# A two-layer convolution and attention network on eight images: position terms of the first image's keys formed without the round trip through DRAM, and its pieces in another order

## The chip, the cores and the metric

The kernel runs on one core of one Trainium2 chip. A core has TensorE (PE, matrix products; its weight loads are shown as PEld), VectorE (DVE, elementwise), ScalarE (ACT, activations and copies), GpSimd (POOL, elementwise by a general processor), SyncE (SP, which here issues most DMAs), sixteen DMA engines, the on-chip memory SBUF and the matrix accumulator PSUM. The metric is the device time of one execution in microseconds (us), lower is better.

## The reference, cut to what matters

Input x is 8 images of 512 channels by 32 x 32, fp32. Layer 0 group-normalises the image, takes a 1x1 convolution to 512 channels (cv1), sends the second half of these through two blocks, each a 3x3 convolution and an attention over the 1024 pixels with four heads of 64 channels, joins everything in a 1x1 convolution (cv2) and adds the input. Layer 1 group-normalises again, takes a depthwise 3x3 and a 1x1 convolution and adds its input. The part that the change touches is the position term r in the attention's keys:

```python
q, k, v = (qkv[:, 0], qkv[:, 1], qkv[:, 2])
r = (rw + rh).reshape(1, HEADS, HD, hw)
logits = jnp.einsum('bhdi,bhdj->bhij', q, k + r) * HD ** (-0.5)
a = jax.nn.softmax(logits, axis=-1)
out = jnp.einsum('bhij,bhdj->bhdi', a, v)
```

rw has one value for each channel and column, rh one for each channel and line, so r is a 1024-element row for each of 256 channels, the same for all eight images. It exists once for each of the two blocks.

## The kernel before, in words

**Staging.** One image is worked on at a time, with all of its 512 channels as four tiles of 128 partitions by 1024 pixels. The pixels lie in "phases": four groups by column modulo 4. All arithmetic is fp32.

**The 3x3 convolutions** are done by a transform method. Weights are transformed once, in the first image: pieces `ta0`, `ta1`, `ta2` make "uplanes" from the raw weights (DVE for 0 and 1, ACT for 2), `ti0`..`ti2` combine them (DVE, tiles `ucomp`) and store them to DRAM (`u_dram`, by SP), `to0`..`to2` scale and store the outer ones (ACT, its own DMA queue). The raw weights of block 0 wait in the tiles `qy`, `kr` and `vt`, those of block 1 in `ht` and `xt`. Then, for every image and block: `d` transforms the input along and across rows (DVE, tiles `vtmp`, `v`, and then `kr`, `vt`, `qy` as the three groups of components), `P` multiplies (six pieces of 32 products, PSUM tiles `ps_c`), `Rc`, `R`, `B`, `E` transform back (ACT copies `c`, DVE tiles `mid`, `sd`, `y`) and `Ez` writes z. `P` takes its transformed weights from a ring of five 1 MB tiles (`wring`); a new ring load is issued on SP when a tile has been used (`ring_load`, `rl`).

**Query, key, value.** `k`, `v` and `q` are products of z with the ring's weights. `ka` (`add_positions`) adds the position rows to the keys while it takes them out of PSUM: DVE reads `ps_qk` and `kr` and writes `kr`. For this `kd` (`load_positions`) has loaded both position tiles from DRAM into `kr`. They come from `rk` (`positions`, line 880 on): four pieces, made in the first image by GpSimd (line 886) and stored by SP to `r_dram`.

**Attention.** 32 steps in a block. In each, `s` makes scores (PSUM `ps_s`, eight matmul instructions), `e` is ACT's exponential into a tile `e`, `p` adds it to `sum` on DVE, `w` multiplies it with the values (`ps_av`). `h` and `z` join halves, `n` and `nr` make the reciprocals of the sums, `ns` spreads them (a DMA, `rw<-r`), `sc` scales z. `m`, `ma`, `mr` close the block, `Q` is the cv2 product.

**Other first-image work.** In the first image's second attention the cv2 and layer-1 weights are combined for later images (`cw`: `combine_more` and `combine_weights`): a load into `ht`, sums on DVE (tiles `scomb`), stores by SP (`q<-ht`, `q<-scomb`, `s<-ht`, `s<-scomb`). `g`..`ga` are group norms, `fo` folds the batch norms.

**What sets the order.** The order is written out by hand. `FIRST` holds the first image's pieces, `HEAD` and `TAIL` those of images 2 to 7, `HEAD` and `LAST` those of image 8. `go` calls them in turn. PE, DVE, ACT and SP are wrapped in `InOrder` (line 94; its calls are recorded at line 104), so each of these four runs its instructions in exactly that order; GpSimd is free within its dependencies. An instruction that waits therefore holds everything behind it on its engine. Temporary tiles (`uplane`, `wtmp`, `ucomp`, `pos`, `scomb`, `e`, `sum`, `mid` and more) share one pool of 11 buffers of 512 KB; a new tile waits until the last reader of an old one is done, and for a stored tile that is its DMA.

Of the kernel before, what the change touches and what calls it, by code (L numbers as in the profile page):

```python
# [12 lines left out]
ALU = mybir.AluOpType  # L13
AX = mybir.AxisListType

P = 128
B, C, F = 8, 512, 32
# [25 lines left out]


FIRST = """
    g*5 gm gd g*2 gv g gp gm gd gb ga gv ga c gp fo gb ga ta0 ga ta0*2 ti0 ta2 fo ta2 c to0 ti0
    to0 c ti0 ta2 c rk*2 rl ca rk ta1*3 rk y ya ti1 ca ti2 to2 ti1*2 y to1 ya ti2 to1 d y*2 ti2
    d*2 ya d to2 rl P Rc d*2 R d*2 P d Rc d kd R d P Rc R ya B d P B P Rc R Rc R P E B Ez B Rc R
    E Ez X ta0 dw k*3 ka k ta0 ka ta0 ti0*2 v ta1 ti0 v*2 q va q qa v va q ta1*2 q qa s e s e p
    to0 s e w to0 s e w*2 p ti1*2 s e p ti1 p s e p w s*2 ta2 e p w e w to1*2 s e w s e p w h p  # L50
    z s ta2 e p ta2 s e ti2 w p w s w e p ti2 s e w p ti2 to2 s*2 e p w to2 e w s e p w s e p rh
    w h z s*2 w e*2 n nr p w s e p w nr s e p w s nr e nc s nr e ns w s p e w*2 p nc s e p w h z
    s p e p s w s*2 e w p e p w sc s e p w*2 e sc s e w*3 h p*2 n z nr*4 ns Q nc*2 K sc dp sc m
    ma mr m ma m*2 ma*2 mr*3 Q d*4 K P*2 kd Rc d*3 R d*3 Rc R d*2 P Rc R B P Rc P Rc R B*2 R E
    Ez B P Rc R E Ez k X k dx k*2 ka v ka v q v*2 va*2 q qa q*2 qa s*2 e s w e p s e p e w s p e
    cw*4 s e w s e p w p s e s p w s p e*2 w cw*2 w*2 p s w h e w z s p s e*2 p w s p g cw e s e
    w s w s p e g p g s w s p e w e g p w g e p h z s w e p s cw*2 w e p n nr*3 w s g e s p w nr
    e s e p s w e ns w g w s e w p h p s e p nc*2 s w e p w s e w s p sc e w s p e p s e p w sc
    w*3 h z*2 n nr Q*2 nr*2 g nr ns sc*2 nc m ma mr nc m ma m mr ma m ma mr gm gd mr Q*2 gv u A
    x u i A x gp i*3 Q gb ga*4 Q im id Q iv A x i ip Q i ib b bm t*2 Q t A x t i*2  # L60
"""

HEAD = """
# [20 lines left out]
"""  # L84

LAST = """
    Q sc*2 nc*2 m ma m*3 ma rg ma mr*2 ma mr*2 Q*2 A rg x i*2 Q im id iv ip ib b bm Q*3 t A x
    i*2 im id t*3 iv ip t ib Q t b Q bm t*3 A t l lr t Q x i*2 Q im lp id t iv ip t A ib t b bm
    Q t*2 A x t l lr x i*2 o lp o*3 im id t*2 o*3 iv ip t o*2 t ib b bm o*5 t o t*2 o t l t*2 lr
    lp t*3 o t*2 o*4 l o lr lp o*6 oa*2 fr f oa*2 fr f o*2 oa*2 o*2 fr oa f oa fr f  # L90
"""


# [31 lines left out]
def fast_kernel(  # L125
# [16 lines left out]
    nc = Engines(tc)  # L142
# [12 lines left out]
    def const_tile(shape, name):  # L155
        return const.tile(shape, F32, tag=name, name=name)

    def work_tile(name):
        return workp.tile([P, HW], F32, tag="work", name=name)

    def big_tile(name):
        return ps_big.tile([P, 2, 512], F32, tag="big", name=name)
# [33 lines left out]
    z = const_tile([P, 2, HW], "z")  # L196

    qy = const_tile([P, 2, HW], "qy")
    kr = const_tile([P, 2, HW], "kr")
# [54 lines left out]
    sc = const_tile([P, NBN], "sc")  # L254
# [19 lines left out]
    dw = v_sb[:, V_DW : V_DW + 9 * KC].rearrange("p (c t) -> p c t", t=9)  # L274
    rw = v_sb[:, V_RW : V_RW + 4 * F].rearrange("p (l m w) -> p l m w", l=2, w=F)
    rh = v_sb[:, V_RH : V_RH + 4 * F].rearrange("p (l m h) -> p l m h", l=2, h=F)
# [7 lines left out]
    def flat(ps):  # L284
        return ps.rearrange("p n f -> p (n f)")
# [5 lines left out]
    def phases(ap):  # L291

        return ap.rearrange("p (r h t) -> p r h t", h=F, t=F // 4)
# [12 lines left out]
    def add(name, *pieces):  # L306
        todo.setdefault(name, []).extend(pieces)
# [104 lines left out]
    def ring_load(n=1):  # L412
        for _ in range(n):
            if not sources:
                continue
            if holds and len(sources) <= holds[0]:
                waiting[0] += 1
                continue
            src = sources.pop(0)
            t = ringp.tile([P, 2048], F32, tag="ring", name="wring")  # L420
            o = t[:, : src[1]]
            if src[1] == 1024:
                o = o.rearrange("p (k o) -> p k o", o=P)
            nc.sync.dma_start(o, src[0])
            ring.append(t)
# [454 lines left out]
    def positions(l, m):  # L880

        t = work_tile("pos")
        full = [P, 4, F, F // 4]
        col = rw[:, l, m, :].rearrange("p (t r) -> p r t", r=4).unsqueeze(2)
        row = rh[:, l, m, :].unsqueeze(1).unsqueeze(3)
        nc.gpsimd.tensor_tensor(phases(t), col.to_broadcast(full), row.to_broadcast(full), ALU.add)
        nc.sync.dma_start(r_dram[l][:, m], t)

    def qkv(l, by_input):


        wt, tiles, values = [], {}, {}

        def weights():
            if not wt:
                wt.append(ring.pop(0)[:, : 6 * C2].rearrange("p (k o) -> p k o", k=2))
            return wt[0]

        def products(m, k):
            w = weights()  # L900
            if m not in tiles:
                tiles[m] = big_tile("ps_qk")
            for n in range(2):
                nc.tensor.matmul(
                    tiles[m][:, n, :],
                    w[:, k, m * P : (m + 1) * P],
                    z[:, k, n * 512 : (n + 1) * 512],
                    start=(k == 0),
                    stop=(k == 1),
                )  # L910

        def load_positions():
            nc.sync.dma_start(kr, r_dram[l])

        def add_positions(m):
            nc.vector.tensor_tensor(kr[:, m, :], flat(tiles.pop(m + 2)), kr[:, m, :], ALU.add)

        def value_products(g, js):
            w = weights()
            if g not in values:  # L920
                values[g] = ps_big.tile([P, 4, C2], F32, tag="big", name="ps_v")
            for j in js:
                jt = 4 * g + j
                for k in range(2):
                    nc.tensor.matmul(
                        values[g][:, j, :],
                        z[:, k, jt * P : (jt + 1) * P],
                        w[:, k, 2 * C2 : 3 * C2],
                        start=(k == 0),
                        stop=(k == 1),  # L930
                    )

        def value_end(g):
            nc.scalar.copy(vt[:, 4 * g : 4 * g + 4, :], values.pop(g))

        def query_end(m):
            nc.scalar.copy(qy[:, m, :], flat(tiles.pop(m)))

        order = [(k, m) for m in (2, 3) for k in range(2)]
        add("k", *[lambda m=m, k=k: products(m, k) for k, m in (sorted(order) if by_input else order)])  # L940
        add("kd", load_positions)
        add("ka", *[lambda m=m: add_positions(m) for m in range(2)])
        add("v", *[lambda g=g, j=j: value_products(g, (j, j + 1)) for g in range(2) for j in (0, 2)])
        add("va", *[lambda g=g: value_end(g) for g in range(2)])
        add("q", *[lambda m=m, k=k: products(m, k) for m in range(2) for k in range(2)])
        todo["q"].append(lambda last=todo["q"].pop(): (last(), ring_load()))
        add("qa", *[lambda m=m: query_end(m) for m in range(2)])
# [402 lines left out]
    for b in range(B):  # L1350
# [26 lines left out]
        for l in range(2):  # L1377
            conv3(l)
            qkv(l, first)
            attention()  # L1380
            cv2m(l)
# [471 lines left out]
```

## Time and profile before

| | us |
|---|---|
| median of 3 runs | 2611.19 |
| lowest, highest | 2610.63, 2613.28 |
| span of the profiled execution | 2610.8 |
| PE busy in it | 2561.2 (98%) |
| DVE busy | 2081.7 (80%) |
| ACT busy | 1185.3 (45%) |
| POOL busy | 101.7 (4%) |

PE is busy in nearly all of the span. An image in the middle takes PE without a break, and the time in which PE stands idle lies in the first image (its start, and its second attention) and at the end of the last one. So the stretches of the first image have to be read one by one: in each, which engine had work, what the idle one waited for, and what was queued ahead of that. The page's totals, and the group means over all images, hide this.

### The profile page before, as it was taken

What the parts mean: (1) busy time and instruction counts of PE and PEld (TensorE: products, weight loads), DVE (VectorE), ACT (ScalarE), POOL (GpSimd) and SP (SyncE); (2) the same over time, 40 slices, a digit from 0 to 9 for tenths busy, and PEclk for the clock granted to TensorE, in tenths of its full rate; (3) what the DMA queues carried; (4) which work ended last, traced back from release to release, by engine and by line L of the source; (5) the groups of instructions that cost most, each with busy time, mean ns of one, the idle gap of its engine ahead of it and who ended that gap; (6) DMA issues with size and microseconds to landing.
All of it is one profiled execution on the core that took longest, in us unless ns stands there. A gap on an engine that the chain in (4) does not pass through costs nothing.

```text
span 2610.8 us, 36350 instructions
## 1 busy us (share of the span) xinstructions
PE 2561.2 (98%) x14806; PEld 1292.4 (50%) x14806; DVE 2081.7 (80%) x2978; ACT 1185.3 (45%) x1523; POOL 101.7 (4%) x71
## 2 busy tenths in 40 slices
PE   6999999999999999999999999999999999999997
PEld 4554464544636346363464634646355453645443
DVE  8875678876898768987788877887788877888657
ACT  3544436353363533635446354453445444453534
POOL 3000001000000000000000000000000000000000
PEclk9999999999999999999999999999999999999999
DMA  8455230332304222151130601306122161312300
GB/s 329 154 200 188 66 136 25 112 143 65 121 25 165 99 73 105 33 209 54 65 122 17 246 17 65 122 17 246 33 77 93 38 225 33 129 42 93 113 17 33
DMA packets 82061, 270.59 MB, mean 104 GB/s; under 512 B 6880, under 2 KB 37344, under 8 KB 65632
## 3 DMA queue, kind: packets, MB, share of 16 engines
q1 hardware_dynamic: 78336, 264.79, 28.4%
q10 hardware_dynamic: 3552, 3.41, 0.4%
q8 instruction: 118, 1.93, 0.3%
q14 instruction: 55, 0.45, 0.0%
HBM read 214.44 MB, written 36.96 MB: 96 GB/s over the span
## 4 chain that ended last, share of the span: by engine, by line
PE 91%; DVE 6%; ACT 1%; DMA 1%; issue 0%; SPq 0%; POOL 0%; ACTq 0%; DVEq 0%
PE ps_av L104 17%; PE ps_s L104 16%; PE ps_c L104 12%; PE ps_cv L104 10%; PE ps_qk L104 8%; PE ps_cv2q L104 8%; PE ps_q L104 6%; PE ps_v L104 4%; PE ps_m L104 4%; PE ps_y L104 4%; PE ps_dn L104 1%; DVE ht L104 1%; ACT qy L104 1%; DVE vtmp L104 1%; DVE mid L104 1%; DVE uplane L104 0%
## 5 line engine op out<-in xcount | busy, mean ns | idle before, releaser
L104 ACT ACTIVATE e<-ps_s 128x1024 f32<-128x1024 f32 x512 | 509.5, 1023 | 291.5 <-PE ps_s L104 264.4
L104 PE MATMUL ps_s<-qy,kr 64*64 64x512 f32 x4096 | 514.9, 593 | 5.8 <-ACT e L104 4.4
L104 DVE TENSOR_TENSOR sum<-sum,e 128x1024 f32<-128x1024 f32 x384 | 475.6, 1239 | 41.5 <-ACT e L104 22.1
L104 PE MATMUL ps_av<-e,vt 64*64 64x512 f32 x4096 | 507.2, 591 | 0.0
L104 DVE SCALAR_TENSOR_TENSOR ht<-xn,v_sb,ht 128x961 f32<-128x961 f32 (+1 forms) x256 | 312.5, 1228 | 8.4 <-ACT ht L104 5.0
L104 PEld LDWEIGHTS ps_s<-qy,kr 64*64 64x64 f32 x4096 | 160.4, 133 | 295.0 <-issue 185.5
L104 PEld LDWEIGHTS ps_av<-e,vt 64*64 64x64 f32 x4096 | 164.8, 133 | 279.1 <-issue 270.5
L104 PE MATMUL ps_qk<-z,wring 128*128 128x512 f32 x512 | 229.7, 596 | 1.8 <-ACT z L104 1.1
L104 DVE TENSOR_TENSOR sum<-e 128x1024 f32<-128x1024 f32 x64 | 78.3, 1223 | 138.7 <-ACT e L104 136.0
L104 ACT COPY c<-ps_c 128x256 f32<-128x256 f32 x96 | 35.6, 371 | 271.6 <-PE ps_c L104 271.6
L104 PEld LDWEIGHTS ps_qk<-z,wring 128*128 128x128 f32 x512 | 95.8, 190 | 117.8 <-issue 100.4
L104 PE MATMUL ps_c<-kr,wring 128*128 128x128 f32 x1024 | 119.8, 279 | 9.1 <-DVE kr L104 9.1
L104 PEld LDWEIGHTS ps_c<-kr,wring 128*128 128x128 f32 x1024 | 119.4, 196 | 17.3 <-DVE kr L104 9.9
L104 DVE RECIPROCAL r<-ps_dn 128x128 f32<-128x128 f32 x128 | 112.9, 924 | 11.2 <-PE ps_dn L104 9.0
L104 PE MATMUL ps_c<-vt,wring 128*128 128x128 f32 x1024 | 118.2, 276 | 1.7 <-ACT c L104 1.7
L104 PE MATMUL ps_c<-qy,wring 128*128 128x128 f32 x1024 | 117.7, 275 | 1.1 <-ACT c L104 0.5
L104 PEld LDWEIGHTS ps_c<-vt,wring 128*128 128x128 f32 x1024 | 116.3, 192 | 2.2 <-ACT c L104 2.0
L104 PE MATMUL ps_cv<-pt,w_sb 128*128 128x512 f32 x256 | 115.9, 604 | 0.8 <-ACT pt L104 0.8
L104 PEld LDWEIGHTS ps_c<-qy,wring 128*128 128x128 f32 x1024 | 115.8, 192 | 1.6 <-issue 0.9
L104 PE MATMUL ps_v<-wring,z 128*128 128x256 f32 x512 | 114.6, 379 | 0.0
L104 PE MATMUL ps_m<-z,wm_sb 128*128 128x512 f32 x256 | 112.5, 592 | 0.0
L104 PE MATMUL ps_y<-pt,w_sb 128*128 128x512 f32 x256 | 112.3, 592 | 0.0
(175 smaller groups left out, 3233.2 us busy)
## 6 DMA issues: line engine op xcount, KB each, us to landing
wring<-u SPq DMA_DIRECT2D x96, 1024.0 KB, 4.9
pt<-in_x SPq DMA_DIRECT2D x32, 512.0 KB, 9.5
kr<-r SPq DMA_DIRECT2D x16, 1024.0 KB, 6.9
rw<-r SPq DMA_DIRECT2D x64, 256.0 KB, 3.4
xt<-in_x SPq DMA_DIRECT2D x32, 512.0 KB, 5.9
out<-xt SPq DMA_DIRECT2D x32, 512.0 KB, 3.3
wring<-q SPq DMA_DIRECT2D x14, 896.0 KB, 5.8
wring<-in_wqkv SPq DMA_DIRECT2D x16, 768.0 KB, 4.8
```

Source lines behind the costliest of these rows:

```text
L104: made = method(*args, **kwargs)
```

## The change

Four things are edited.

1. In the first image (`by_input` is true there), `kd` and `ka` give way to `ka` (`columns`) and `kp` (`lines`). `columns` runs on DVE and adds the broadcast rw to the keys as it takes them out of PSUM; `lines` runs on GpSimd and adds the broadcast rh to `kr` in place. The first image no longer reads the position tiles.
2. `positions` is made by DVE instead of GpSimd.
3. `FIRST` is in another order. The four `rk` stand in the second attention (before: in the first 35 us). The group norm at the start takes six `g` before its first `gm`; the weight transforms, the first `d`s and the back transforms stand in another sequence; `cw*3` stands before the query products instead of after the first scores; the last two `cw` of the second attention and several `g` stand elsewhere.
4. `LAST` is in another order: the same pieces, mostly depthwise taps `t` and the range check `rg` at other places.

```diff
 FIRST = """
-    g*5 gm gd g*2 gv g gp gm gd gb ga gv ga c gp fo gb ga ta0 ga ta0*2 ti0 ta2 fo ta2 c to0 ti0
-    to0 c ti0 ta2 c rk*2 rl ca rk ta1*3 rk y ya ti1 ca ti2 to2 ti1*2 y to1 ya ti2 to1 d y*2 ti2
-    d*2 ya d to2 rl P Rc d*2 R d*2 P d Rc d kd R d P Rc R ya B d P B P Rc R Rc R P E B Ez B Rc R
-    E Ez X ta0 dw k*3 ka k ta0 ka ta0 ti0*2 v ta1 ti0 v*2 q va q qa v va q ta1*2 q qa s e s e p
...
-    Ez B P Rc R E Ez k X k dx k*2 ka v ka v q v*2 va*2 q qa q*2 qa s*2 e s w e p s e p e w s p e
-    cw*4 s e w s e p w p s e s p w s p e*2 w cw*2 w*2 p s w h e w z s p s e*2 p w s p g cw e s e
-    w s w s p e g p g s w s p e w e g p w g e p h z s w e p s cw*2 w e p n nr*3 w s g e s p w nr
...
+    g*6 gm gd gv g gp g gb gm gd ga gv ga c gp fo gb c ta0 ga ta0 ga ta0 ti0 fo ta2 to0*2 c
+    ti0*2 ca ta2*2 c rl ca ta1*3 ti2 ti1 to1 d ti1 d y ya to1 ti1 y ya ti2 to2 d y ti2 d to2 rl
+    ya y d*2 ya d P Rc R P d*3 Rc R d*2 P Rc R B P Rc R B*2 P*2 Rc R E Ez B Rc R E Ez k*2 X k dw
+    ta0 ka k kp ka ta0*2 v kp ti0 v va ti0 v ti0 q v va ta1 q ta1 qa q*2 qa ta1 s e s e p to0 s
...
+    Ez Rc B*2 R E Ez k X dx k*3 ka*2 kp*2 v*2 q v*2 va*2 cw*3 rk cw q*2 qa q qa s*2 e*2 p s e p
+    w s e w s p cw*2 e s e w s e p rk p w s e p*2 s e w s e g*2 w*2 p w h z s e w cw s e p*2
+    cw*2 rk s e w*2 s e w s*2 p e rk w p s e g w p g p s*2 e g w g e*2 p w h z p s w e g p w n
...
 """
...
-        nc.gpsimd.tensor_tensor(phases(t), col.to_broadcast(full), row.to_broadcast(full), ALU.add)
+        nc.vector.tensor_tensor(phases(t), col.to_broadcast(full), row.to_broadcast(full), ALU.add)
...
+        def columns(m):
+            col = rw[:, l, m, :].rearrange("p (t r) -> p r t", r=4)
+            nc.vector.tensor_tensor(
+                phases(kr[:, m, :]),
+                phases(flat(tiles.pop(m + 2))),
+                col.unsqueeze(2).to_broadcast(full),
+                ALU.add,
+            )
+
+        def lines(m):
+            row = rh[:, l, m, :].unsqueeze(1).unsqueeze(3)
+            kk = phases(kr[:, m, :])
+            nc.gpsimd.tensor_tensor(kk, kk, row.to_broadcast(full), ALU.add)
...
-        add("kd", load_positions)
-        add("ka", *[lambda m=m: add_positions(m) for m in range(2)])
+        if by_input:
+            add("ka", *[lambda m=m: columns(m) for m in range(2)])
+            add("kp", *[lambda m=m: lines(m) for m in range(2)])
+        else:
+            add("kd", load_positions)
+            add("ka", *[lambda m=m: add_positions(m) for m in range(2)])
```

More of the change, by code (lines that the diff above doesn't have):

```diff
@@ L45 @@
 FIRST = """
-    g*5 gm gd g*2 gv g gp gm gd gb ga gv ga c gp fo gb ga ta0 ga ta0*2 ti0 ta2 fo ta2 c to0 ti0
-    to0 c ti0 ta2 c rk*2 rl ca rk ta1*3 rk y ya ti1 ca ti2 to2 ti1*2 y to1 ya ti2 to1 d y*2 ti2
-    d*2 ya d to2 rl P Rc d*2 R d*2 P d Rc d kd R d P Rc R ya B d P B P Rc R Rc R P E B Ez B Rc R
-    E Ez X ta0 dw k*3 ka k ta0 ka ta0 ti0*2 v ta1 ti0 v*2 q va q qa v va q ta1*2 q qa s e s e p
-    to0 s e w to0 s e w*2 p ti1*2 s e p ti1 p s e p w s*2 ta2 e p w e w to1*2 s e w s e p w h p
-    z s ta2 e p ta2 s e ti2 w p w s w e p ti2 s e w p ti2 to2 s*2 e p w to2 e w s e p w s e p rh
@@ L52 @@
-    w h z s*2 w e*2 n nr p w s e p w nr s e p w s nr e nc s nr e ns w s p e w*2 p nc s e p w h z
-    s p e p s w s*2 e w p e p w sc s e p w*2 e sc s e w*3 h p*2 n z nr*4 ns Q nc*2 K sc dp sc m
-    ma mr m ma m*2 ma*2 mr*3 Q d*4 K P*2 kd Rc d*3 R d*3 Rc R d*2 P Rc R B P Rc P Rc R B*2 R E
-    Ez B P Rc R E Ez k X k dx k*2 ka v ka v q v*2 va*2 q qa q*2 qa s*2 e s w e p s e p e w s p e
-    cw*4 s e w s e p w p s e s p w s p e*2 w cw*2 w*2 p s w h e w z s p s e*2 p w s p g cw e s e
-    w s w s p e g p g s w s p e w e g p w g e p h z s w e p s cw*2 w e p n nr*3 w s g e s p w nr
@@ L58 @@
-    e s e p s w e ns w g w s e w p h p s e p nc*2 s w e p w s e w s p sc e w s p e p s e p w sc
-    w*3 h z*2 n nr Q*2 nr*2 g nr ns sc*2 nc m ma mr nc m ma m mr ma m ma mr gm gd mr Q*2 gv u A
-    x u i A x gp i*3 Q gb ga*4 Q im id Q iv A x i ip Q i ib b bm t*2 Q t A x t i*2
+    g*6 gm gd gv g gp g gb gm gd ga gv ga c gp fo gb c ta0 ga ta0 ga ta0 ti0 fo ta2 to0*2 c
+    ti0*2 ca ta2*2 c rl ca ta1*3 ti2 ti1 to1 d ti1 d y ya to1 ti1 y ya ti2 to2 d y ti2 d to2 rl
+    ya y d*2 ya d P Rc R P d*3 Rc R d*2 P Rc R B P Rc R B*2 P*2 Rc R E Ez B Rc R E Ez k*2 X k dw
@@ new lines @@
+    ta0 ka k kp ka ta0*2 v kp ti0 v va ti0 v ti0 q v va ta1 q ta1 qa q*2 qa ta1 s e s e p to0 s
+    e p w to0 s e w*2 ti1 s e p ti1*2 p s e p w s to1 s e p w e p w s w to1 ta2 e s e w h p z
+    ta2 s e p ta2 s ti2 e w*2 s e w ti2 to2 ti2 s e w s e to2 w s e w s e w s e rh p w p*5 h z
+    s*2 w e*2 n s e w p s p w nr e p w nr*2 s e nc s nr e ns p w s e p w*2 nc s e p w h z s e s
+    w s*2 p*2 e w p e*2 p sc p w sc s w e p w s e p w*3 h z n nr*4 ns nc sc Q K m ma sc dp mr
+    m*2 ma mr m ma mr ma mr d*4 Q nc K d*3 P d P Rc R d*2 Rc R d*2 P Rc R P*2 Rc B R B P Rc R E
@@ new lines @@
+    Ez Rc B*2 R E Ez k X dx k*3 ka*2 kp*2 v*2 q v*2 va*2 cw*3 rk cw q*2 qa q qa s*2 e*2 p s e p
+    w s e w s p cw*2 e s e w s e p rk p w s e p*2 s e w s e g*2 w*2 p w h z s e w cw s e p*2
+    cw*2 rk s e w*2 s e w s*2 p e rk w p s e g w p g p s*2 e g w g e*2 p w h z p s w e g p w n
+    nr s e nr p w g s e s p w nr e s e w p w*2 s nr p e s e w h ns p s e p nc*2 s w e p w s e p
+    w s e p w s sc e p s e p w sc w*3 h z n nr*2 Q nr*2 ns z Q sc*2 nc m*2 ma mr ma mr m ma nc m
+    ma mr gm mr gd Q gv u A Q x u i A x i gp i*2 Q gb ga*4 Q im id Q iv A Q x ip i*2 ib b bm t*3
@@ L61 @@
+    Q A t x i*2
 """
@@ L86 @@
 LAST = """
[L87 to L90, printed above, removed]
+    Q sc nc*2 m ma m sc m*2 ma rg ma mr*2 ma mr*2 Q*2 A x Q i*2 im id rg iv ip ib b bm Q*2 t A x
+    i*2 Q im id t*3 iv ip t ib t Q t b Q bm t Q*2 t A t l lr x i*2 im t lp id t iv ip t A ib t b
+    bm Q t A x t*2 l lr o x i*2 o lp o*2 im t id t o*3 iv ip t*2 o ib b t*3 bm t o*4 t*2 o*4 l t
+    lr lp t*4 l lr lp o*10 oa o*2 oa fr f oa*2 fr f o*3 oa o oa fr oa f oa fr f
 """
@@ L910, in products @@
                 )
+        full = [P, 4, F, F // 4]
         def load_positions():
```

## The prediction

> **What bounds the kernel now.** I read the page's busy line and slices first, then the windows of the first image, then the timeline inside the two windows where PE stands, then what SP and POOL did there.
>
> ```profile
> PE 2561.2 (98%) x14806; PEld 1292.4 (50%) x14806; DVE 2081.7 (80%) x2978; ACT 1185.3 (45%) x1523; POOL 101.7 (4%) x71
> ...
> PE   6999999999999999999999999999999999999997
> ```
>
> PE is the bound, and only the first and the last slice are clearly open: 2610.8 - 2561.2 = 49.6 us idle in all. The change touches the first image and the order of the last, so the windows view of image one is next (window, length, busy time of PE, PEld, DVE, ACT and POOL with counts, granted clock, DMA share, GB/s):
>
> ```profile
> 0.00:43.68 43.68, 31.60 (x72) 14.73 (x72) 34.86 (x56) 15.75 (x18) 21.98 (x18) 1.00 0.79 300
> 43.68:52.73 9.05, 0.00 (x0) 0.00 (x0) 7.79 (x10) 4.50 (x7) 0.00 (x0) 0.75 1.05 390
> 52.73:78.72 25.99, 24.84 (x192) 24.46 (x192) 22.73 (x49) 5.30 (x13) 0.00 (x0) 0.89 1.00 365
> 223.10:288.10 65.00, 60.47 (x530) 21.03 (x529) 52.21 (x64) 36.33 (x41) 0.00 (x0) 0.95 0.49 158
> ```
>
> PE does nothing for 9.05 us before the first transformed products, while DVE is busy for 7.79 of it and DMA is full; in the next 26 us DMA stays full and the clock is at 0.89. The second attention takes 65.0 us with 4.5 us without PE work; the first one, of the same products, ran from 100.72 to 158.9 (58.2). The timeline names the causes (start, duration, engine, instruction, count, and in brackets the idle time ahead and its releaser):
>
> ```profile
> 18.74 5.71 POOL L886 TENSOR_TENSOR pos<-v_sb 128x1024 f32<-128x1024 f32 x2
> 15.50 1.29 DVE L104 TENSOR_TENSOR uplane<-wtmp,qy 128x512 f32<-128x512 f32 x2
> 19.36 5.64 DVE L104 TENSOR_TENSOR uplane<-wtmp,vt 128x512 f32<-128x512 f32 x2
> 26.18 2.41 DVE L104 TENSOR_TENSOR sc<-sc,v_sb 128x24 f32<-128x24 f32 x1
> 37.62 3.40 DVE L104 SCALAR_TENSOR_TENSOR uplane<-vt,wtmp 128x512 f32<-128x512 f32 x2
> 50.66 1.29 DVE L104 TENSOR_TENSOR v<-vtmp 128x512 f32<-128x512 f32 x2 [1.14 <-DMA u<-uplane]
> 52.73 10.14 PE L104 MATMUL ps_c<-kr,wring 128*128 128x128 f32 x64 [9.06 <-DVE kr L104]
> 54.88 11.47 SPq L104 DMA_DIRECT2D wring<-u  x4
> ```
>
> PE waits for DVE to write kr. On that chain DVE loses time wherever POOL makes pos: the pair that takes 1.29 us alone took 5.64, a one-sided 24-element sum 2.41 where its neighbours take about 0.2, and a later pair 3.40. After the idle time the 64 products took 10.14 us, where the same 64 at 178.02 take 7.38.
>
> ```profile
> 230.42 3.33 SPq L104 DMA_DIRECT2D q<-ht  x6
> 237.85 0.55 SPq L104 DMA_DIRECT2D ht<-in_w  x1
> 243.82 0.69 DVE L104 TENSOR_TENSOR scomb<-ht 128x512 f32<-128x512 f32 x1 [5.49 <-DMA ht<-in_w]
> 250.43 1.94 ACT L104 ACTIVATE e<-ps_s 128x1024 f32<-128x1024 f32 x2 [5.67 <-DMA s<-scomb]
> 251.51 1.98 PE L104 MATMUL ps_s<-qy,kr 64*64 64x512 f32 x8 [4.45 <-ACT e L104]
> ```
>
> In the second attention DVE, whose order is fixed, stands at a weight sum whose load was queued on SP behind fourteen stores; the e buffers behind it don't come free, ACT waits for one, and PE waits for ACT.
>
> **What the Trainium skill says.** "GPSIMD Engine Reference", Key points: GpSimd shares its SBUF interfaces with VectorE and contends with DVE instructions that have two SBUF inputs or run in a two-port mode. The trace agrees: 5.64 against 1.29. "TensorE: Matmul & The Clock Gate", What's actually happening: after an idle window the array runs at half clock until it has been busy for one. The trace agrees in kind: 10.14 against 7.38 after 9.06 us idle, and 8-product groups at 1.98 against about 1.04 after 4.45. "DMA: Bandwidth & Descriptors", Issuing engines are not separate DMA queues: DMAs of SP and ACT share the same sixteen engines. The trace shows share 1.00 to 1.05 while both issue.
>
> **The change, part by part**
>
> *Norm order.* Before, the first pair's scale (nb at 14.68) stood on DVE behind the second pair's small work, though POOL's input for it existed from about 12.9. Afterwards it comes first, so the first cv1 products start about 0.8 us earlier (0 to 1.2): y ends at 42.9 instead of 43.68.
>
> *POOL's pos out of the start.* DVE gets back 5.64 - 1.29 = 4.35, 2.41 - 0.2 = 2.2 and 3.40 - 1.29 = 2.1, together 8.65 us, and waits for stores of 0.43 + 0.69 + 1.14 = 2.3 that DMA traffic makes long. By its new order from 15.0: three ta0 (each 0.68 + 1.29, overlapping to 1.93) 5.8, a ti0 1.2, fo 1.0, two ti0 2.5, three ta1 6.0, five ti 6.0, vtmp, v and the first kr pair 3 x 1.29: the first pair at about 41, the other two at about 43.5, needed from about 44.7 on. That is before y ends or just behind it, so the products start at about 42.9 instead of 52.73: 9.8 us, and with a warm clock 10.14 - 7.2 = 3.0 us more. Bound below: DVE's full 11 us of loss is not all recovered if the stores, still 8 MB or so of traffic, keep it waiting; then the start gains 7 to 10 in all.
>
> *DMA of the start.* Gone are four stores r<-pos of 0.5 MB and the first image's two kr<-r of 1 MB, of which three MB lie before 79 us; at the 365 to 390 GB/s shown, 3.1 MB is about 8 us of full DMA. The r<-pos also stood on SP ahead of two wring<-u, and SP waited 2.7 us for POOL there. Ring loads are what holds PE once DVE doesn't: the third is issued near 44 and lands after some 7.7 us as those in this window do, at about 51.5, where PE is done with its first 64 at 50.0: a gap of 1.5. The four 32-product pieces then take 3.6 each: 65.8. The tail to the second z is 4.4 us in the trace (78.86 to 83.27): 70.1 instead of 83.27. **Gain at the start: 13.2**, that is 0.8 + 9.05 + 3.0, plus about 1.9 from gaps and slow pieces in 52.73 to 78.72, less the gap of 1.5.
>
> *columns and lines.* Two DVE sums for each block take the place of two add_positions of the same size (1.23 each, PSUM and SBUF in); with a broadcast second operand I take 1.22, bounds 1.1 to 1.4. Two POOL sums for each block are new. The nearest row is pos itself, alone 2.87 us and 3.47 beside DVE; the page "GPSIMD Engine Reference", Elementwise cycle accounting, gives a two-input sum as 1.96 times DVE's time, an estimate of 2.4. I take 2.9, and 2.4 to 6 as the bounds, since in place and 4-dimensional. They follow columns, about 73 to 79 in block one; the first scores come at about 87.5, eleven us behind the first of them, and the second half of the keys is needed sixteen steps later. In block two they lie at about 209 to 215, the scores at about 217 after the shift. DVE may lose up to 4.2 us while POOL runs; value and query products (11 us) hide most of that, and I charge 0.5.
>
> *rk in the second attention.* Four DVE sums at about 1.2 (same size, both operands broadcast; 1.1 to 1.4), 4.9 us, one of them before the scores. Sums of q weights of 3.0 us leave the attention for the query products, so DVE there has about 54 us in 58, 93%. The window 410:470 of a later image has DVE at 56.03 of 60 with PE at 59.92, so this load hides. Their four stores (0.5 MB) join SP's queue; image two reads them at about 385, 130 us later: hidden.
>
> *cw*3 ahead of the queries.* The load ht<-in_wpw was queued behind a ring load that waited for the last q (both issued at 223.2 to 223.5). Afterwards it is issued about 19 us before the first scores S and lands at S - 11; sums until S - 8, stores until S - 4, the next load lands at S + 3 (before: S + 20.7, from 223.07), its sums at S + 7; the second load lands at about S + 19 and is summed at S + 21. By then no step of e waits for a buffer. The 4.45 us of idle and the 8-product groups at the half clock behind it (2.4) go: 65.0 - 58.2 = 6.8. I take 6.5; 0 to 6.8.
>
> *LAST.* PE's order but for a piece or two is the same, and the end is bound by DVE's taps back to back; their number is unchanged. 0, bounds -0.5 to +0.5.
>
> *Other orders.* Between 158 and 202 PE loses 1.9 us before, and the new orders of transforms may shift it by 1: charged 0.5.
>
> Sum: 13.2 + 6.5 - 0.5 - 0.5 = 18.7. On the profiled span 2610.8 that is 2592.1; the runs' median is 0.4 above the span: 2592.5.
>
> **Rivals**
>
> *The start is bound by DMA or ACT instead.* For it: DMA at 1.05 just where PE stands, and the weight stores and ring loads remain. Against: PE was released by DVE's kr, and 3 MB go. Then the start gains 7 to 10 rather than 13: 2594.5 to 2598.5.
>
> *The second attention still stalls.* For it: four position stores and DVE sums are put where the stall is, and a temporary tile is held until its store lands; with 11 buffers an e may wait again. Against: the load comes 18 us earlier. Then 2 to 6 less: 2595 to 2599.
>
> *Nothing much happens*, if DVE's loss at the start was not POOL's doing but the traffic's, and DMA then bounds; the stall stays as well: 2604 or more.
>
> *Slower: lines on POOL hold the scores.* The first scores need the first sum. Slack is about 11.5 us beyond 2.9, so it decides from about 14.5 us for one sum; to eat 18.7 in two blocks it would take 14.5 + 9.4 = 24 us each, eight times pos. Then 2611 or above. The two pos rows speak against it.
>
> **How the numbers follow.** Full gain 17 to 21: 0.56, 2590 to 2594.5. Start only in part: 0.20. Second attention stalls: 0.12. Over 21 (the gaps in the products go as well): 0.05, down to 2588. Little: 0.04. Slower: 0.03, and half of "little" can't be told from no change: 0.2%, 5.2 us, is about what a measurement of this kernel can tell. The range 2588 to 2600 holds the first four. Faster 0.95, same 0.03, slower 0.02 (a slower case smaller than 0.2% counts as same).
>
> **What would show it.** First ps_c at about 43 with no 9 us ahead of it; DVE's uplane pairs at 1.29 throughout; PEclk near 1 from 43 to 70; kr<-r x14; pos on DVE near 1.2; lines on POOL near 2.9 with no PE wait behind them; the second attention in about 58 us, no e waiting for a store of scomb; the last 70 us unchanged. The forecast fails if ring loads gate PE after 50, if ACT's transforms hold the DMA stores late, or if POOL's lines take over 10 us.

## The result and the profile after

| | before | after |
|---|---|---|
| median of the runs, us | 2611.39 (6 runs) | 2597.26 (6 runs) |
| lowest, highest | 2610.63, 2613.28 | 2596.68, 2597.82 |
| span of the profiled execution | 2610.8 | 2595.2 |

The ratio is 0.9944, with a 95% interval of 0.9932 to 0.9957: faster by 14.1 us. The forecast was 2592.5 with a range of 2588 to 2600, so the way and the range hold, and the gain is three quarters of the 18.9 that was forecast (2611.4 - 2592.5). On the profiled spans, for which the sum was made, it is 15.6 against 18.7. The case that was given the most weight, a full gain of 17 to 21, did not come; the range holds because it takes in the smaller gains too.

The page of the changed kernel (busy line, slices of PE):

```profile
PE 2558.3 (99%) x14806; PEld 1291.6 (50%) x14806; DVE 2084.2 (80%) x2982; ACT 1185.6 (46%) x1523; POOL 98.0 (4%) x71
...
PE   8999999999999999999999999999999999999997
```

Only the first slice of PE has moved, as a gain in the first image should look. The windows of that image (window, length, busy time of PE, PEld, DVE, ACT and POOL with counts, granted clock, DMA share, GB/s), cut where PE's work changes:

```profile
0.00:44.02 44.02, 32.64 (x72) 15.28 (x73) 35.79 (x69) 20.51 (x24) 9.94 (x14) 1.00 0.91 343
44.02:52.41 8.39, 7.31 (x65) 7.14 (x64) 7.36 (x14) 2.57 (x7) 0.00 (x0) 1.00 1.04 371
52.41:67.57 15.16, 14.53 (x128) 14.34 (x128) 14.33 (x35) 2.75 (x7) 0.00 (x0) 1.00 0.90 325
212.34:272.31 59.97, 59.46 (x530) 22.25 (x529) 55.16 (x60) 36.47 (x41) 0.00 (x0) 1.00 0.45 149
```

The 9.05 us without PE work are gone, the clock is full in all four windows, and the second attention takes 60.0 us instead of 65.0. The timeline of the changed kernel (start, duration, engine, instruction, count, and in brackets the idle time ahead and its releaser) answers to the one shown of before:

```profile
19.42 1.29 DVE L105 TENSOR_TENSOR uplane<-wtmp,vt 128x512 f32<-128x512 f32 x2
...
21.89 0.18 DVE L105 TENSOR_TENSOR sc<-sc,v_sb 128x24 f32<-128x24 f32 x1
...
29.75 1.29 DVE L105 SCALAR_TENSOR_TENSOR uplane<-vt,wtmp 128x512 f32<-128x512 f32 x2
...
44.02 7.31 PE L105 MATMUL ps_c<-kr,wring 128*128 128x128 f32 x64
52.41 7.38 PE L105 MATMUL ps_c<-vt,wring 128*128 128x128 f32 x64 [1.08 <-DMA wring<-u]
```

The three DVE instructions that took 5.64, 2.41 and 3.40 us beside GpSimd take 1.29, 0.18 and 1.29. PE goes from the y products to ps_c without a gap, and what holds it next is a ring load, for 1.08 us.

Where the 15.6 us come from is read by setting the start of the same instruction in both traces side by side:

| instruction | before | after | gain so far |
|---|---|---|---|
| first product of the image (ps_cv) | 14.42 | 13.59 | 0.8 |
| first ps_c, block 1 | 52.73 | 44.02 | 8.7 |
| first ps_qk, block 1 | 78.72 | 67.57 | 11.2 |
| first scores, block 1 | 100.72 | 89.30 | 11.4 |
| first ps_c, block 2 | 178.02 | 166.22 | 11.8 |
| first scores, block 2 | 223.07 | 212.34 | 10.7 |
| cv2 product behind the second attention | 288.09 | 272.31 | 15.8 |
| end | 2610.8 | 2595.2 | 15.6 |

So the start gives 11.2 (11.4 by the first scores), the second attention 5.05 (65.02 against 59.97), the stretch before its scores takes about 1 back, and the seven other images nothing.

### The profile page after: what moved, and what is told of

Read it like the earlier page. It is cut to its first block, busy times and chain, and to the rows that moved or that the text cites. A ratio compares the mean times of both kernels' runs of the same rounds, so it can differ in the third digit from the quotient of the medians.

```text
span 2595.2 us, 36342 instructions
## 1 busy us (share of the span) xinstructions
PE 2558.3 (99%) x14806; PEld 1291.6 (50%) x14806; DVE 2084.2 (80%) x2982; ACT 1185.6 (46%) x1523; POOL 98.0 (4%) x71
## 3 DMA queue, kind: packets, MB, share of 16 engines
HBM read 212.34 MB, written 36.96 MB: 96 GB/s over the span
## 4 chain that ended last, share of the span: by engine, by line
PE 92%; DVE 4%; ACT 2%; DMA 1%; issue 0%; ACTq 0%; POOL 0%; SPq 0%; DVEq 0%
PE ps_av L105 16%; PE ps_s L105 16%; PE ps_c L105 12%; PE ps_cv L105 11%; PE ps_qk L105 8%; PE ps_cv2q L105 8%; PE ps_q L105 6%; PE ps_v L105 4%; PE ps_m L105 4%; PE ps_y L105 4%; PE ps_dn L105 1%; ACT qy L105 1%; DVE ht L105 1%; DVE vtmp L105 0%; DVE mid L105 0%
```

## The experiments

The theory after the result: (1) the start was held by DVE, which GpSimd slowed; (2) the second attention was held by a load behind fourteen stores; (3) what the forecast promised beyond that was lost because a ring load now holds the start, and because DVE is full in the second attention. The rivals: the transfers that went away made the start faster; other new places cured the attention; GpSimd, not DVE, should have kept the position tiles. Each kernel below is the changed one with one edit, and its time is compared with the changed kernel's 2597.3. The intervals of the ratios are about 2 to 3.5 us wide to each side, and the kernel before, measured again beside these runs, had medians from 2611.6 to 2612.2. So differences of a few us are read from the landmarks of one profile each and only supported by the medians, and a difference of less than about 1 us between two medians is not told from none. Three landmarks of each profile carry the reading (start of the first ps_c, start of the first scores, length of the second attention):

| kernel | median, us | first ps_c | first scores, block 1 | second attention | ratio to before, 95% interval |
|---|---|---|---|---|---|
| before | 2611.4 | 52.73 | 100.72 | 65.02 |  |
| changed | 2597.3 | 44.02 | 89.30 | 59.97 | 0.9944 (0.9932 to 0.9957) |
| sums back | 2608.5 | 42.91 | 89.65 | 70.82 | 0.9988 (0.9982 to 0.9995) |
| rows at the start, GpSimd | 2606.7 | 55.15 | 101.97 | 57.95 | 0.9982 (0.9974 to 0.9990) |
| rows at the start, VectorE | 2600.9 | 51.06 | 96.19 | 57.95 | 0.9958 (0.9944 to 0.9972) |
| extra stores | 2603.1 | 43.60 | 94.86 | 60.01 | 0.9969 (0.9957 to 0.9981) |
| norm back | 2597.9 | 45.11 | 89.54 | 59.95 | 0.9947 (0.9933 to 0.9960) |
| rows by GpSimd in the attention | 2596.5 | 43.75 | 89.67 | 58.86 | 0.9942 (0.9929 to 0.9956) |
| even columns | 2596.0 | 44.27 | 88.96 | 58.48 | 0.9936 (0.9922 to 0.9949) |
| rows late | 2596.7 | 43.84 | 89.25 | 57.95 | 0.9945 (0.9932 to 0.9959) |
| rows late, even columns | 2594.4 | 43.90 | 88.66 | 57.95 | 0.9937 (0.9923 to 0.9950) |
| rows later, even columns | 2594.2 | 42.79 | 88.74 | 57.96 | 0.9936 (0.9922 to 0.9949) |
| last image back | 2597.9 | 43.99 | 89.14 | 59.94 | 0.9950 (0.9936 to 0.9964) |

### The start: GpSimd, VectorE's work, or transfers

**Rows at the start, by GpSimd**

```diff
-    ti0*2 ca ta2*2 c rl ca ta1*3 ti2 ti1 to1 d ti1 d y ya to1 ti1 y ya ti2 to2 d y ti2 d to2 rl
+    ti0*2 ca ta2*2 c rk*2 rl ca rk ta1*3 rk ti2 ti1 to1 d ti1 d y ya to1 ti1 y ya ti2 to2 d y ti2 d to2 rl
...
-        nc.vector.tensor_tensor(phases(t), col.to_broadcast(full), row.to_broadcast(full), ALU.add)
+        nc.gpsimd.tensor_tensor(phases(t), col.to_broadcast(full), row.to_broadcast(full), ALU.add)
```

(the four rk are taken out of the second attention)

> The changed kernel, with the four position tiles made by GpSimd again and at their old places in the first 35 us (they are stored, but the first image doesn't read them). Theory (GpSimd slows VectorE there by about 9 us): DVE's uplane pairs reach 3 to 6 us again, PE idles 6 to 9 us before the first transformed products and loses up to 3 us of clock, the attention gets back up to 2: time 2603 to 2608. Rival (the removed loads of positions were what counted, not the contention): below 2600.

2606.68 us (2605.38 to 2610.29). DVE in this profile:

```profile
19.29 5.64 DVE L105 TENSOR_TENSOR uplane<-wtmp,vt 128x512 f32<-128x512 f32 x2
...
26.11 2.44 DVE L105 TENSOR_TENSOR sc<-sc,v_sb 128x24 f32<-128x24 f32 x1
...
36.96 3.51 DVE L105 SCALAR_TENSOR_TENSOR uplane<-vt,wtmp 128x512 f32<-128x512 f32 x2
...
48.42 1.23 DVE L105 TENSOR_TENSOR ucomp<-ucomp,uplane 128x1024 f32<-128x1024 f32 x1 [4.48 <-DMA r<-pos]
```

The three slow instructions are back, at the same places and lengths. The last line shows a cost that was not in the prediction: a position tile keeps its buffer until its store lands, and DVE waits 4.48 us for one. The first scores come at 101.97, later than in the kernel before (100.72): with GpSimd making the tiles there, nothing of the start's gain is left, though the first image no longer loads positions and the pieces stand in the new order. The reverse, the old order without the tiles, was not run, so what the new order of the transforms adds to the gain stays open.

**Rows at the start, by VectorE** (the same order, without the second edit)

> The changed kernel, with the four position tiles made by VectorE but at the old places in the first 35 us. They take 4 x 2.0 = 8.0 us of DVE ahead of kr, of which some 2.5 us are slack; the 2 MB of stores come back as in the run with GpSimd. Theory: PE idles about 5 us before the first transformed products, and up to 3 us of clock are lost; the second attention gets 2 us back: time 2600 to 2604, a little less than with GpSimd, since the DVE work is as long as GpSimd's contention but adds no wait for it. If transfers were the cause, this run and the one with GpSimd are equal and DVE waits for stores.

2600.91 us (2600.03 to 2603.01), within the expectation. DVE makes the four tiles in 7.8 us (three in the first line, one in the second) and nothing beside them is slow:

```profile
25.50 5.86 DVE L105 TENSOR_TENSOR pos<-v_sb 128x1024 f32<-128x1024 f32 x3
...
37.17 1.98 DVE L105 TENSOR_TENSOR pos<-v_sb 128x1024 f32<-128x1024 f32 x1
```

Against the run with GpSimd the stores and the places are the same, and the first scores come 5.8 us sooner (96.19 against 101.97). GpSimd's contention and the buffers that it holds thus cost 5.8 us more than doing the work on the contended engine itself. The contention is the smaller part of that: the three slow instructions lose 8.8 us to it (4.35 + 2.26 + 2.22), one more than the 7.8 that DVE's own tiles take. The larger part goes with the waiting for stores: DVE waits 4.48 us behind a position tile with GpSimd, and not at all with VectorE.

**Extra stores.** Neither run says what the transfers did alone. This one stores 2 MB from a weight tile into an unused place, and adds no work for an engine:

```diff
-    ti0*2 ca ta2*2 c rl ca ta1*3 ti2
+    ti0*2 ca ta2*2 c xs*2 rl ca xs ta1*3 xs ti2
...
+            extra = dram.tile([P, 4, HW], F32, tag="extra", name="extra")
+            add("xs", *[
+                lambda i=i: nc.sync.dma_start(
+                    extra[:, i], w1_sb.rearrange("p a b -> p (a b)")[:, :HW]
+                )
+                for i in range(4)
+            ])
```

> The changed kernel, with four stores of 0.5 MB from a weight tile into an unused place in DRAM, put into SP's queue where the position stores stood before, without any work on DVE or GpSimd. It measures the transfers' part of the start alone. Theory A (the ring load at 43.6 us, which lands at 52.4 and holds PE for 1.1 us, is held by full DMA): 2 MB at about 370 GB/s delay it, or the weight stores that DVE and SP wait for, by up to 5.5 us: 2599 to 2603. Theory B (the gain at the start was DVE's alone, and the stores are hidden): 2597 to 2598.

2603.1 us (2600.96 to 2605.15): Theory A. PE in this profile:

```profile
43.60 1.95 PE L105 MATMUL ps_c<-kr,wring 128*128 128x128 f32 x16
46.61 5.62 PE L105 MATMUL ps_c<-kr,wring 128*128 128x128 f32 x48 [1.06 <-ACT kr L105]
56.59 8.77 PE L105 MATMUL ps_c<-vt,wring 128*128 128x128 f32 x64 [4.35 <-DMA wring<-u]
```

ps_c starts as early as ever, but the next ring load comes later: its group starts at 56.59 instead of 52.41, and runs 1.4 us longer behind the idle time. The first scores are 5.6 us late. SP's issues, first of the changed kernel and then of this one, show why:

```profile
43.63 12.07 SPq L105 DMA_DIRECT2D wring<-u  x4
```

```profile
47.22 13.12 SPq L105 DMA_DIRECT2D wring<-u  x4
```

SP, which issues in order, comes to the load later, because the weight stores ahead of it land later (at 46.58 against 43.62). Of the 4.2 us by which the group is late, 3.6 are the issue and 0.6 the load itself. So the transfers were a limit of their own, half as large as the start's gain of 11.4. The costs don't add: stores alone cost 5.6, stores and 7.8 us of DVE work 6.9, stores and GpSimd 12.7. The stores alone would thus have cost half the gain; GpSimd's tiles without their stores were not run, so what the contention costs by itself is read from the traces only. The two 1 MB loads of positions, which both kernels of the start's rows also lack, were not tried by themselves.

**Norm back**

```diff
-    g*6 gm gd gv g gp g gb gm gd ga gv ga c gp fo gb c ta0
+    g*5 gm gd g*2 gv g gp gm gd gb ga gv ga c gp fo gb c ta0
```

(both lines cut behind the first `ta0`)

> The changed kernel, with the group norm of the start in its old order. The first cv1 products start about 0.8 us later. Theory (when they get fast is set by when the clock is granted, at steps of about 3.4 us whose place differs between runs): the end of the y products moves by anything from -1.4 to +1.4, and the median by 0 to +0.8: 2597.3 to 2598.1. Rival (the prediction's step as it stood): +0.8, 2598.1.

2597.85 us (2597.39 to 2598.85). The first product starts 0.98 us later (14.57 against 13.59) and ps_c 1.09 us later (45.11 against 44.02), but ps_qk starts only 0.25 us later (67.82 against 67.57): PE's wait for the ring load falls from 1.08 to 0.20. The new order of the norm is worth about a quarter of a microsecond in the profile, because its gain ends in a wait for a transfer. The profile with late tiles and the later places says the same from the other side: ps_c at 42.79, ps_qk at 67.63.

### The second attention: the load, and VectorE's load

**Sums back**

```diff
-    Ez Rc B*2 R E Ez k X dx k*3 ka*2 kp*2 v*2 q v*2 va*2 cw*3 rk cw q*2 qa q qa s*2 e*2 p s e p
-    w s e w s p cw*2 e s e w s e p rk p w s e p*2 s e w s e g*2 w*2 p w h z s e w cw s e p*2
+    Ez Rc B*2 R E Ez k X dx k*3 ka*2 kp*2 v*2 q v*2 va*2 rk q*2 qa q qa s*2 e*2 p s e p
+    w s e w s p cw*4 e s e w s e p rk p w s e p*2 s e w cw*2 s e g*2 w*2 p w h z s e w cw s e p*2
```

> The changed kernel, with the first four cw pieces of the second attention put back behind the first scores; everything else as changed. Theory (the late load of the weight sums was what held the e buffers): the stall returns, the second attention takes about 65 us again instead of 60.0, time about 2602 (2600.5 to 2604). Rival (the stall went because of the other new places of p, g and rk, or because the start's transfers are gone): no change, 2596.5 to 2598.

2608.48 us (2607.63 to 2610.72), above the expected range: the stall returns, twice as large as expected. (The edit also moves the two cw behind the first four.) ACT and PE in this profile:

```profile
239.33 1.02 ACT L105 ACTIVATE e<-ps_s 128x1024 f32<-128x1024 f32 x1 [8.61 <-DMA r<-pos]
...
240.41 1.99 PE L105 MATMUL ps_s<-qy,kr 64*64 64x512 f32 x8 [7.69 <-ACT e L105]
```

The load ht<-in_wpw is issued at 213.18 again, behind a ring load, DVE waits 4.02 us for the load that follows the q stores, and ACT waits for a buffer. The releaser is now a position tile's store: SP issues in order, so a position store that stands behind sums that wait for a load keeps its buffer too. In the changed order ACT waits 1.19 us for such a store and 1.47 for one of scomb, and PE shows no wait behind either. The attention of 70.8 us is 10.9 longer, which is nearly all of the 11.2 us. The place of these cw pieces is what cures the stall. With the tiles in this attention it costs more than it did before (65.02 without them); the old place without the tiles was not run in the new order.

**Rows late**

```diff
-    w s e p w s sc e p s e p w sc w*3 h z n nr*2 Q nr*2 ns z Q sc*2 nc m*2 ma mr ma mr m ma nc m
-    ma mr gm mr gd Q gv u A Q x u i A x i gp i*2 Q gb ga*4
+    w s e p w s sc e p s e p w sc w*3 h z n nr*2 Q nr*2 ns z Q sc*2 nc m*2 ma mr rk ma mr m ma nc rk m
+    ma mr gm mr gd Q rk gv u A Q x u i rk A x i gp i*2 Q gb ga*4
```

(the second line of each pair is cut behind `ga*4`; the four rk are taken out of the attention)

> The changed kernel, with the four position tiles (still VectorE, 2.0 us each) moved out of the second attention to the cv2 products behind it, where DVE is half idle. Theory (DVE is full in the second attention, and its late sums hold ps_dn): the waits at ps_dn go, the attention takes about 58.2 us, time 1.5 to 2 less than the changed kernel: 2595.2 to 2595.9. Rival (the e buffers or the stores hold the attention): 2597, as the changed kernel.

2596.72 us (2596.22 to 2599.34), above the expected range: the attention falls to 57.95, the waits at ps_dn are gone, and yet the time falls by 0.5 only. What the changed kernel has at ps_dn, and what its DVE does ahead of it:

```profile
240.36 2.04 DVE L105 TENSOR_TENSOR pos<-v_sb 128x1024 f32<-128x1024 f32 x1
...
245.82 1.05 PE L105 MATMUL ps_dn<-sum,ones 128*32 128x512 f32 x4
247.24 1.05 PE L105 MATMUL ps_dn<-sum,ones 128*32 128x512 f32 x4 [0.37 <-DVE sum L105]
...
270.70 1.67 PE L105 MATMUL ps_dn<-sum,ones 128*32 128x512 f32 x8
```

and, of the kernel with the rows late, behind the attention:

```profile
245.76 1.07 PE L105 MATMUL ps_dn<-sum,ones 128*32 128x512 f32 x8
...
288.69 2.84 PE L105 MATMUL ps_cv<-qy,wring 128*128 128x512 f32 x6 [1.66 <-DVE qy L105]
```

Eight of these products take 1.07 us where nothing holds them. In the changed kernel the first eight take from 245.82 to 248.29 and the second 1.67, so DVE's late sums cost it 2.0 us at its two groups of ps_dn; in the late places the tiles stand in front of a qy sum, and PE waits 1.66 us there. A half-idle engine still has instructions that somebody waits for.

**Even columns**

```diff
+    rwp = const_tile([P, 4 * F], "rwp").rearrange("p (l m r t) -> p l m r t", l=2, m=2, r=4)
...
+        for l in range(2):
+            for m in range(2):
+                nc.gpsimd.tensor_copy(rwp[:, l, m], rw[:, l, m, :].rearrange("p (t r) -> p r t", r=4))
...
-        col = rw[:, l, m, :].rearrange("p (t r) -> p r t", r=4).unsqueeze(2)
+        col = rwp[:, l, m].unsqueeze(2)
...
-            col = rw[:, l, m, :].rearrange("p (t r) -> p r t", r=4)
+            col = rwp[:, l, m]
```

> The changed kernel, with the column values copied once into the phase order (four small GpSimd copies), so that columns and positions read them at a step of one element instead of four. Theory A (the step of four makes these sums 2.0 us instead of 1.2): both fall to about 1.23, the second attention's DVE gets 3.2 us back and the waits at ps_dn shrink: 2595 to 2596.5. Theory B (the broadcast or the four-dimensional pattern makes them 2.0): they stay near 2.0, time unchanged.

2595.99 us (2594.72 to 2596.35): Theory A. The tile view of pos (duration in ns, least/median/most, first and last start), first of the changed kernel, then of this one:

```profile
L105 DVE TENSOR_TENSOR pos<-v_sb x4: 1977/2039/2059, 204.9 to 240.4; 128x1024 f32<-128x1024 f32 x4
```

```profile
L105 DVE TENSOR_TENSOR pos<-rwp,v_sb x4: 1216/1216/1217, 204.4 to 237.9; 128x1024 f32<-128x1024 f32 x4
```

The same sum over 1024 elements takes 1.22 us where the columns lie side by side and 2.04 where they are read four elements apart; the columns sums fall from 1.99 to 1.22 likewise. The row operand, which repeats one element eight times, costs nothing. The attention takes 58.48.

**Rows by GpSimd in the attention** (only the engine of positions is put back)

> The changed kernel, with the four position tiles made by GpSimd instead of VectorE, at their new places in the second attention. Theory (GpSimd takes time from VectorE wherever it runs beside two-input sums): each tile takes 2.4 to 3.5 us on POOL and the sums beside it get up to 2 us longer, so DVE is relieved little; the second attention stays at 59 to 62 us, time 2596.5 to 2599.5. Rival (DVE's own 2.0 us each are dearer than the contention): attention 58.3, time 2595.5.

2596.54 us (2595.54 to 2598.53), attention 58.86. POOL takes 2.45 us for each tile. Two of the tiles, and DVE's sums beside them:

```profile
228.21 2.45 POOL L887 TENSOR_TENSOR pos<-v_sb 128x1024 f32<-128x1024 f32 x1 [12.04 <-PE ps_av L105]
229.16 2.58 DVE L105 TENSOR_TENSOR sum<-e 128x1024 f32<-128x1024 f32 x1
...
233.42 2.45 POOL L887 TENSOR_TENSOR pos<-v_sb 128x1024 f32<-128x1024 f32 x1 [2.77 <-PE ps_av L105]
232.26 4.69 DVE L105 TENSOR_TENSOR sum<-sum,e 128x1024 f32<-128x1024 f32 x2
```

A sum alone takes 1.2 us. Both stretches of sums end 1.1 us behind a POOL tile (231.74 behind 230.66, 236.95 behind 235.87), so DVE's sum stood still until the tile was done. Another tile, from 213.72 to 216.17, ran while DVE waited for the first exponentials, and cost it nothing. The theory's time was 2596.5 to 2599.5 and its attention 59 to 62, the rival's 2595.5 and 58.3: the time is at the theory's edge, and the attention lies between the two, 1.1 us shorter than with DVE's own 2.0 us sums. So here GpSimd is the better of the two by the attention's length; the medians, 0.7 apart, can't settle it. With even columns DVE is the cheaper by 0.4 us of attention and 0.6 in the medians, about what the runs differ among themselves.

**Rows late with even columns, and rows later**

> Both: the position tiles behind the second attention, and the columns read at a step of one element. If the two act on the same thing (DVE's load in the second attention), the gains don't add: about 0.3 to 0.7 below the better of the two alone, from the shorter columns sums ahead of the value products: 2595.0 to 2595.7. If they act on different things they add: 2594.3 or less.

2594.39 us (2593.96 to 2597.01), 1.6 below the better of the two alone and more than was expected: 2.9 below the changed kernel, where the two alone are 0.5 and 1.3 below. So they do not act on the same thing only: the attention is at 57.95 with late rows already, so what the even columns add lies elsewhere, in the first scores (88.66 against 89.25 and, in block 2, 211.09 against 212.28) and behind the attention, where the wait for qy falls from 1.66 to 0.18. In the traces the gains add up: at the first scores of image two (391.46 in the changed kernel) the even columns alone are 2.4 ahead, the late rows alone 0.1, both 2.8. The medians (1.3, 0.5 and 2.9) agree with this to about 1 us and no better.

For the second of the two kernels, the places of rk (the edits for the even columns not shown again):

```diff
-    ma mr gm mr gd Q gv u A Q x u i A x i gp i*2 Q gb ga*4 Q im id Q iv A Q x ip i*2 ib b bm t*3
-    Q A t x i*2
+    ma mr gm mr gd Q gv u A Q x u i A x i gp i*2 Q gb ga*4 Q im id rk*2 Q iv A Q x ip i*2 ib b bm t*3
+    rk*2 Q A t x i*2
```

> The position tiles still later, two and two in the gaps of DVE that the first run with late tiles shows at 302 to 308 and 318 to 322 us, and the columns at a step of one element. Theory: the 1.66 us (0.18 with the even columns) for which PE waited for a qy sum behind a position tile go, the rest as there: 2593.5 to 2594.5. Rival (SP's queue, in order, now holds a ring load behind a position store that waits for DVE): a new wait for wring behind 300 us, 2595 or more.

2594.23 us (2593.87 to 2595.11), attention 57.96, and no wait behind it: the theory's value, and no measurable gain over the run before, since only 0.18 us were left. These two are the fastest kernels here, their medians 3 us below the changed one's.

### The last image

```diff
-    Q sc nc*2 m ma m sc m*2 ma rg ma mr*2 ma mr*2 Q*2 A x Q i*2 im id rg iv ip ib b bm Q*2 t A x
...
+    Q sc*2 nc*2 m ma m*3 ma rg ma mr*2 ma mr*2 Q*2 A rg x i*2 Q im id iv ip ib b bm Q*3 t A x
...
```

> The changed kernel, with the last image in its old order. The prediction had this part at 0, between -0.5 and +0.5. Theory: the end is bound by the same number of depthwise taps on DVE, so 2596.8 to 2597.8, and the last image's length in the profile differs by under 0.5 us. Rival (its order gave a part of the gain, or took one): 2598.5 or more, or 2596 or less.

2597.85 us (2597.12 to 2599.9), 0.05 outside the theory's range and not distinguishable from 2597.26. From the last ps_dn to the end the two profiles take 112.65 (2482.95 to 2595.6) and 112.62 us (2482.58 to 2595.2). The order of the last image is worth nothing that these runs can show.

## Why the prediction was right, and where its sizes were off

**POOL out of the start: right, with its mechanism.** The three slow instructions fell to 1.29, 0.18 and 1.29. The first kr pair was written from 39.8 to 41.1 (forecast: at about 41), PE had no gap, and 64 products took 7.31 instead of 10.14 us. The traces show more of the mechanism than the forecast read in them. The other two tiles of before, beside the lines that the prediction shows:

```profile
25.08 3.47 POOL L886 TENSOR_TENSOR pos<-v_sb 128x1024 f32<-128x1024 f32 x1 [0.63 <-DVE uplane L104]
...
36.96 2.91 POOL L886 TENSOR_TENSOR pos<-v_sb 128x1024 f32<-128x1024 f32 x1 [8.41 <-DMA r<-pos]
```

The 24-element product (it reads two SBUF tiles, and is not one-sided as the prediction has it) starts beside the first of these and ends at 28.59, where the tile ends at 28.55. The pair that took 3.40 us starts at 37.62 beside the second, which ends at 39.87, and the pair then needs 1.15 us more, about its length alone. By these ends VectorE did not run slower beside a tile: its sum waited for the end of the tile. It went the other way too: the tiles that the prediction calls alone at 2.87 us ran beside the pair that took 5.64, and in the attention, where no such sum was in their way, the tiles took 2.45.

**The norm: right at its place, wrong at its worth.** The first product came 0.83 us earlier, but the y products ended at 44.02 and not at 42.9. In both traces the first products run at half clock, and full speed begins at 17.5 us before and at 19.4 after; in the profiles of these runs it begins at anything from 16.8 to 20.6 us. In the run with the sums back it began at 16.9, and the y products ended at 42.91, as forecast; its ps_qk still started at 67.94. The forecast carried the 0.8 through to the end; the runs show it absorbed, first by the clock, whose steps lay differently in each profile, and then by the ring load.

**The ring load: the step that fixed the start was 0.9 us short.** The forecast had its products at 51.5, with 7.7 us for the load; it landed at 52.3, 8.65 us from its issue at 43.63 (DMA share 1.04), and the products started at 52.41. From that place all else followed at the forecast's pace: the products end at 66.9 (65.8), and the second z is written at 71.2, where the forecast had 70.1 and the trace of before 83.3. The gain there is 12.0 against 13.2. The rival in which DMA bounds the start, given 2 chances in 10, holds in part: 1.08 us of wait remain, and the run with extra stores shows that with 2 MB more it would have been the case. (The prediction's last sentence counts a ring load that holds PE after 50 us as a failure, while its own sum has one, of 1.5 us.)

**columns and rk: wrong beyond their bounds.** Forecast 1.22 us each, bounds 1.1 to 1.4; measured 1.99 and 2.04. The DVE rows that the forecast went by had no operand of this step. The Trainium skill had a price for something near it, and the forecast did not use it: "Vector Engine (DVE) Microarchitecture Reference", 5.2 Measured stream behaviour on trn2, says that a port keeps its full rate only where elements come in runs of at least two adjacent words, and gives 1.73 ns per column with one source that hops 4 KiB at every element, and more for small steps than for large ones. An estimate from that is 1024 x 1.73 ns and the page's 75 ns an instruction, 1.85 us; the trace agrees in kind, with 2.04, and 1.22 once the elements lie side by side. The consequence is the attention: DVE had 3.3 us more than planned (4 x 0.82), was full (9.76 to 9.96 us of each 10 in the windows from 222 to 262), and gave ps_dn its sums late. The gain was 5.05 and not 6.5; the run with even columns gets it (65.02 - 58.48 = 6.5), as the step had it.

**lines: better than forecast.** Three of the four took 1.97 us and one 2.40, against 2.9; the estimate of 2.4 from the page "GPSIMD Engine Reference" was nearer than the row of pos, which ran beside DVE. In block one a sum of uplane stood still beside the second of them (2.34 us instead of 0.68), which cost PE nothing. PE waited 0.35 us behind them in each block, for a columns sum and not for POOL. The slower rival had no ground: nothing waited for POOL.

**cw*3 and LAST: right.** The stall is gone, though not each wait of e, as the forecast had it (1.47 and 1.19 us remain, and PE does not wait for them), and it comes back where the place is put back; the last image is unchanged to 0.03 us.

**The two charges of 0.5.** From the second z of block 1 to the first scores of block 2 the forecast gave back 1.0; the traces give back 1.3 (12.0 to 10.7). About half of the last microsecond is the step of columns: with even columns the stretch from the first ps_c of block 2 to the scores is 45.5 us, against 46.1 changed and 45.05 before. Together the span misses 3.1 us: 1.2 at the start, 0.3 here, 1.45 in the attention and 0.2 behind it.

**From span to median.** The sum was made against 2610.8, and the median was put 0.4 above. But a run is 1.8 us longer than its own span in both kernels (2612.56 and 2610.8; 2597.06 and 2595.2), and the profiled run of before was 1.2 us above the median of its runs. This is 1.4 us of the difference between 15.6 and 14.1: a span should be compared with the run that it belongs to.

## What to carry to other kernels

A helper engine that stops a full one while it runs relieves it only where it runs while the full one waits anyway: compare how long the full engine's instructions are while the helper runs with how long they are alone, and set that, with the buffers that the helper holds, against doing the work on the full engine. Here that spoke for VectorE at the start and, before its operand was made even, for GpSimd in the attention. Where a start has two limits, here DVE and the transfers, taking one away shows the other, so the forecast needs the next wait as much as the one removed. When an operand's step is not in the trace, its duration is not in the trace either, and has to be looked up or bounded for itself.

## What the runs showed of the hardware

VectorE's fp32 sum over 1024 elements took 1.22 us with operands of step one and broadcasts, and 2.04 us with a broadcast operand read at a step of four elements (16 bytes). TensorE's clock records show full speed beginning anywhere from 16.8 to 20.6 us in kernels whose first product starts between 13.4 and 14.6: a microsecond won just there may or may not be kept. The later stretches at half clock in these records last 3.4, 6.8 or 10.2 us. Beside a GpSimd sum of two operands, VectorE sums of 1.2 us took up to 2.58, and 4.69 for two; in each case read here they ended 0.04 to 1.2 us behind the GpSimd instruction, as if they had stood still until it was done.
